# Last stage of a spectral layer in the matrices' place, its addend loaded at once, and the first matrices ahead of the token points

## Chip, cores, metric

The kernel runs on one core of a Trainium2 chip. The metric is the device time of one execution in microseconds; the median of three runs of the kernel before is 1634.19 us (1628.76 to 1636.43). Profiles come from one further execution each.

## What is computed

Two layers on an image `x` of 4 x 56 x 56 x 128 in float32. The first is neighbourhood attention with a residual. The second works on the same values as 4 sequences of 3136 tokens: a linear attention with a residual, then a spectral mixer with a residual. The change touches only the mixer, cut here to its core:

```python
t = t + attn(ln(t))
u = ln(t)
# one of four scales (here: all tokens, or the first half, ...) is picked by argmax(log_weights + gumbel)
Uf_p = rfft(u, n=8192);  Uf_m = rfft(u * sign, n=8192)
U_plus  = irfft(Vf * Uf_p)[:, :sl]          # 16 filters phi
U_minus = irfft(Vf * Uf_m)[:, :sl] * sign
out = einsum('btkd,k,kde->bte', U_plus, sigma**0.25, Mpp)
    + einsum('btkd,k,kde->bte', U_minus, sigma**0.25, Mpm)
t = t + out + autoregressive_part(u)
```

## The kernel before

**Phases.** `layers` computes the attention layers, the normalised tokens, the autoregressive part and everything that the spectral part needs. It leaves in DRAM: `td`, the result so far (what the last stage adds to), `xd`, the tokens transformed along rows, `vd`, the transformed filters, and `wd`, the filters' matrices. Its order of instructions on all engines is written out by a planner of its own. `spectral_layer` (L1419) then does the convolution as products between transforms, and `onto_the_rest` (L1680) transforms back along rows and adds the result to `td`. A second copy of all three stands under an `If` that these inputs do not take.

**The spectral layer's order.** There are 42 row frequencies `m1`, grouped in `UNITS`: one, then twenty pairs, then one. Only TensorE's order is written out (`tc.manual_schedule(engines={PE})`); on the other engines and queues the compiler orders instructions by priority and readiness. The step `step(s)` finishes unit `s-1` and prepares unit `s`:

- `load_tokens(m1)` (L1478) loads `xm` from `xd` by four DMAs on SP's queue; `points(m1)` turns it into points by 16 matmuls (32 records, L1490), which DVE, ScalarE and GpSimd copy into one of three `us` tiles (L1499 to L1503).
- `matrices(u, t, n)` (L1521) mixes the 16 x 2 filters' matrices `mats` with the filters' values `v` to the unit's matrices, which DVE and ScalarE copy into `gt` (L1531).
- `product` (L1541) multiplies points and matrices; ScalarE copies to `ys` (L1633).
- `regroup` stores `ys` to `yd` and loads it back as `yg` in another order (L1554 and L1560), `columns` transforms back along columns by 8 matmuls (L1569), ScalarE and DVE copy the two halves to `zs` (L182 and L184), and `store_columns` stores `zs` to `zd` (L1584). These DMAs are on SP's queue.

Before the first step, `mats` (2 MB) is loaded from `wd` by four DMAs on SP's queue (L1433), among the first loads of `v`, `tok` and `back` (`tables_of`, L1463). The first step loads the tokens of `m1 = 0` and 1, makes the points of `m1 = 0`, and then the matrices of unit 0; the second step begins with the first 32 matmul records of the next unit's matrices and then the first product.

The last frequency's chain has nothing after it in the layer: product, `ys`, `yd`, `yg`, `columns`, `zs`, `zd`.

**SBUF of the layer.** The pools `tabs`, `sp` and `sp1` lie one on the other. `sp1` holds what lives through the whole layer: `mats` (16 KB a partition), `gt` (112 KB) and three `us` (32 KB). All pools are freed together when the layer ends.

**The last stage.** `onto_the_rest` opens the pools `fin` and `ps_o`. It zeroes `onto` and the upper 64 rows of eight `z` tiles of 16 KB a partition (four sets of two halves `q`; L1687 and L1697, on DVE and GpSimd). Its eleven steps take 1, 1, 2, 4, 4, 4, 4, 4, 2, 1, 1 columns of the image from each half:

- two DMAs on ScalarE's queue load `tl` from `td` (L1709), 56 rows each, and two on SP's queue load the two `z` from `zd` (L1711), 84 rows from row 0;
- per column, four matmuls (8 records, L1719) with `onto` as weights give a PSUM tile `po` of 128 x 512, of which four rotate;
- DVE adds it, masked, to `tl` in two halves (L1728);
- two DMAs on ScalarE's queue store `tl` to the output (L1733).

Of the kernel before, what the change touches and what calls it, by code (L numbers as in the profile page):

```python
# [57 lines left out]
NS, BR = 2, H // 2  # L58
N1, N2, NM = 42, W, W // 2
# [74 lines left out]
def hybrid_kernel(  # L134
# [39 lines left out]
    hmask = keep.tile([P, 1], F32, name="hmask")  # L174
# [1244 lines left out]
    def spectral_layer():  # L1419


        with ExitStack() as ph:
            tabs = ph.enter_context(tc.tile_pool(name="tabs", bufs=2))
            sp = ph.enter_context(tc.tile_pool(name="sp", bufs=2))
            sp1 = ph.enter_context(tc.tile_pool(name="sp1", bufs=1))
            ps_g = ph.enter_context(tc.tile_pool(name="ps_g", bufs=1, space=bass.MemoryType.PSUM))


# [1 line left out]
            mats = sp1.tile([P, NQE, GE // NQE, C], F32, name="mats")  # L1430
            by_group = wd.rearrange("k (t g i) d -> g k t (i d)", t=NQE, g=NG)
            for g in range(NG):
                nc.sync.dma_start(  # L1433
                    mats[32 * g : 32 * (g + 1)].rearrange("k t i d -> k t (i d)"), by_group[g]
                )

# [151 lines left out]
            def bank():  # L1588
                turn[0] = (turn[0] + 1) % 8
                return ps_g.tile([P, 512], F32, tag=f"g{turn[0]}", name="pg")  # L1590
# [3 lines left out]
            def load_to(m1):  # L1594
                for m in range(len(xms), min(m1, N1 - 1) + 1):
                    xms[m] = load_tokens(m)
# [13 lines left out]
            def step(s):  # L1610


                one = UNITS[s - 1] if s else []
                two = UNITS[s] if s < len(UNITS) else []
                turns = NM // 4
                free = MQ * len(one)

                order = list(range(free, NQE)) + list(range(free)) if two else []
                need = lambda t: -(-NMQ * (t + 1) // 4) if t < free else 0
                done = 0  # L1620

                def make():
                    if order and need(order[0]) <= done:
                        t = order.pop(0)
                        for n in range(len(two)):
                            matrices(s, t, n)

                def use(q, ns):

                    py = bank().rearrange("p (n c) -> p n c", c=C)  # L1630
                    for i, n in enumerate(ns):
                        product(py[:, i], s - 1, us_of(one[q]), q, n)
                    nc.scalar.copy(ys[:, ns[0] : ns[-1] + 1], py[:, : len(ns)])  # L1633

                if not one:
                    load_to(1)
                    points(0)
                    while order:
                        make()
                elif len(one) == 1 and two:  # L1640
                    ys = sp.tile([P, turns, C], F32, name="ys")
                    for n in range(turns):
                        make()
                        use(0, [n])
                        done += 1
                        if n == 3:
                            points(two[0])
                    ygs[one[0]] = regroup(one[0], ys)
                    make()
                    points(two[1])  # L1650
                else:
                    waiting = list(ygs)
                    for q in range(len(one)):
                        ys = sp.tile([P, turns, C], F32, name="ys")
                        for n in range(0, turns, 2):
                            last = n + 1 == turns
                            if last and q == 0 and two:
                                points(two[0])
                            if last and q == len(one) - 1:
                                if q:  # L1660
                                    waiting.append(one[0])
                                for m1 in waiting:
                                    results(m1)
                            use(q, [n] if last else [n, n + 1])
                            done += len(range(n, min(n + 2, turns)))
                            make()
                        ygs[one[q]] = regroup(one[q], ys)
                    if len(two) == 2:
                        points(two[1])
                assert not order  # L1670

            with tc.manual_schedule(engines={mybir.EngineType.PE}):
                for s in range(len(UNITS) + 1):
                    if s + 1 < len(UNITS):
                        tables_of(UNITS[s + 1][0])
                    step(s)
                for m1 in list(ygs):
                    results(m1)

    def onto_the_rest():  # L1680

        with ExitStack() as ph:
            fin = ph.enter_context(tc.tile_pool(name="fin", bufs=4, reuse_waits="tile"))
            ps_o = ph.enter_context(tc.tile_pool(name="ps_o", bufs=4, space=bass.MemoryType.PSUM))

            onto = fin.tile([P, NS, 64], F32, name="onto", bufs=1)
            nc.vector.memset(onto, 0.0)  # L1687
            nc.scalar.dma_start(
                onto[: 2 * N1, :, :H], table["onto"].rearrange("p (s h) -> p s h", s=NS)
            )  # L1690
            zs = [
                [fin.tile([P, 4, NS, B * C], F32, name=f"z{q}{i}", bufs=1) for q in range(2)]
                for i in range(4)
            ]
            for i in range(4):
                for q, e in enumerate((nc.vector, nc.gpsimd)):
                    e.memset(zs[i][q][64:], 0.0)  # L1697
            rows_in = td.rearrange("b (h w) c -> h b w c", w=W)
            rows_out = ot.rearrange("b (h w) c -> h b w c", w=W)

            steps = (1, 1, 2, 4, 4, 4, 4, 4, 2, 1, 1)
            assert sum(steps) == W // 2
            for n, wc in enumerate(steps):
                w0 = sum(steps[:n])
                tl = fin.tile([P, B, max(steps), C], F32, name="tl")
                zin = []
                for q in range(2):
                    ws = slice(q * BR + w0, q * BR + w0 + wc)
                    nc.scalar.dma_start(tl[64 * q : 64 * q + H, :, :wc], rows_in[:, :, ws])  # L1709
                    z = zs[n % 4][q]  # L1710
                    nc.sync.dma_start(  # L1711
                        z[: 2 * N1, :wc], zd[ws].rearrange("w p s b e -> p w s (b e)")
                    )
                    zin.append(z)
                for i in range(wc):
                    po = ps_o.tile([P, B, C], F32, name="po2")
                    for s in range(NS):
                        for q in range(2):
                            nc.tensor.matmul(  # L1719
                                po[64 * q : 64 * (q + 1)].rearrange("p b c -> p (b c)"),  # L1720
                                onto[:, s],
                                zin[q][:, i, s],
                                start=(s == 0),
                                stop=(s == NS - 1),
                            )
                    for q in range(2):
                        at = slice(64 * q, 64 * q + H)
                        nc.vector.scalar_tensor_tensor(  # L1728
                            tl[at, :, i], po[at], hmask[at], tl[at, :, i], ALU.mult, ALU.add
                        )  # L1730
                for q in range(2):
                    ws = slice(q * BR + w0, q * BR + w0 + wc)
                    nc.scalar.dma_start(rows_out[:, :, ws], tl[64 * q : 64 * q + H, :, :wc])  # L1733

    unfit = keep.tile([1, 1], mybir.dt.int32, name="unfit")
    layers(False, unfit)
    bad = nc.values_load(unfit)
    spectral_layer()
    onto_the_rest()
    with tc.If(bad > 0):  # L1740
        layers(True, None)
        spectral_layer()
        onto_the_rest()


# [52 lines left out]
```

## Time and profile before

| | |
|---|---|
| median of the runs | 1634.19 us |
| the profiled execution's own time | 1643.69 us |
| its span, first to last instruction | 1641.8 us |
| TensorE busy in the span | 1436.1 us (87%) |
| DVE, ScalarE, GpSimd busy | 1015.0, 757.9, 411.8 us |
| bytes moved by DMA | 207.22 MB, mean 126 GB/s |
| the layer's first load (v) issued | 747.90 us |
| the first points' matmul | 769.14 us |
| end of the last product's copy to ys | 1488.5 us |
| first tl issue | 1500.76 us |
| last z issue | 1628.33 us |

A row of a group reads: line, engine, operation, output and inputs by the program's names, shape, count, then busy microseconds in all, mean nanoseconds of one, and the idle time of the engine before them with what ended it. `PEld` is the loading of weights, which overlaps the matmuls. `SPq` and `ACTq` are the queues of SyncE and ScalarE, that is, the issuing of DMAs, which is not counted as busy time. In the chain of waits each line is a start, a duration and what the time went to; a line that begins with DMA lasts from the end of the issue to what the landing released. The DMA share is the mean busy share of the core's 16 DMA engines. The last stage's matmuls as a group:

```
L1719 PE MATMUL po<-z,onto 128*64 128x512 f32 x224 | 76.6, 723 | 58.5 <-DMA z<-zd 57.4
```

### The profile page before, as it was taken

To read this page: it belongs to the slowest core of one execution; us is meant where nothing else is said; L and a number is where in the kernel's file an instruction comes from. 1 tells how busy PE (TensorE), PEld (TensorE's weight loads), DVE (VectorE), ACT (ScalarE), POOL (GpSimd) and SP (SyncE) were. 2 spreads that over 40 slices of the span, in tenths; PEclk is the share of its full clock that TensorE was granted. 3 is DMA by queue.
4 is the path that set the end of the run, shared out by engine and by line. 5 is a ranking of instruction groups with operands and counts; after the bars stand their busy time and mean duration, and the time that the engine had idled before them with its cause. 6 is when DMAs were issued, how large, how long until landed. Compare 5 with 4: busy or idle time off the path is not lost.

```text
span 1641.8 us, 60848 instructions
## 1 busy us (share of the span) xinstructions
PE 1436.1 (87%) x26361; PEld 1115.2 (68%) x26361; DVE 1015.0 (62%) x2069; ACT 757.9 (46%) x1610; POOL 411.8 (25%) x813
## 2 busy tenths in 40 slices
PE   4887879889999999883999999999999999992566
PEld 3665658756876776562888888888888888880212
DVE  3775668777876777541766666666666666643324
ACT  2333445346635534342666655666566556640000
POOL 5135327433754464240010011001010101003000
PEclk9698999999999999996999999999999999995788
DMA  6455455744434244257144444444444454435997
GB/s 174 106 109 105 89 86 109 162 122 118 117 111 125 66 121 124 74 157 202 48 113 119 106 123 126 127 108 125 122 126 108 121 132 115 107 93 139 225 252 238
DMA packets 274388, 207.22 MB, mean 126 GB/s; under 512 B 104704, under 2 KB 241056, under 8 KB 274112
## 3 DMA queue, kind: packets, MB, share of 16 engines
q1 hardware_dynamic: 261154, 189.63, 45.1%
q10 hardware_dynamic: 12958, 13.61, 3.1%
q8 instruction: 209, 3.42, 0.9%
q14 instruction: 67, 0.55, 0.1%
HBM read 115.52 MB, written 87.64 MB: 124 GB/s over the span
## 4 chain that ended last, share of the span: by engine, by line
PE 66%; DMA 14%; POOL 7%; DVE 6%; SPq 4%; issue 2%; ACT 1%; POOLq 0%; DVEq 0%; ACTq 0%
PE pg L1521 18%; PE pg L1541 17%; PE pg L1490 5%; PE results L1185 4%; PE scores L1155 3%; PE pg L1569 3%; PE bk L828 3%; SPq L230 2%; DMA z<-zd 2%; DMA tl<-td 2%; DMA out_dram<-tl 2%; PE bk L887 2%; PE bk L733 2%; PE bk L703 2%; PE bk L501 2%
## 5 line engine op out<-in xcount | busy, mean ns | idle before, releaser
L1531 DVE COPY gt<-pg 128x448 f32<-128x448 f32 x672 | 372.9, 617 | 225.6 <-PE pg L1521 225.5
L1531 ACT COPY gt<-pg 128x448 f32<-128x448 f32 x672 | 313.6, 555 | 101.3 <-PE pg L1521 101.1
L1521 PE MATMUL pg<-v,mats 32*128 32x224 f32 (+1 forms) x5632 | 308.9, 356 | 0.0
L1541 PE MATMUL pg<-gt,us 128*32 128x128 f32 x9408 | 297.7, 277 | 1.3 <-DVE gt L1531 1.3
L1541 PEld LDWEIGHTS pg<-gt,us 128*32 128x32 f32 x9408 | 256.5, 138 | 51.8 <-DVE gt L1531 45.4
L1521 PEld LDWEIGHTS pg<-v,mats 32*128 32x128 f32 x5632 | 250.5, 187 | 30.0 <-issue 28.5
L1502 POOL COPY us<-us 128x448 f32<-128x448 f32 x42 | 23.5, 560 | 667.0 <-DVE us L1499 611.9
L1171 ACT ACTIVATE e<-scores 126x768 f32<-126x768 f32 (+1 forms) x140 | 107.6, 769 | 116.8 <-PE scores L1155 93.3
L1175 DVE TENSOR_TENSOR e<-e,relb 126x768 f32<-126x768 f32 (+1 forms) x140 | 138.1, 987 | 23.7 <-ACT e L1171 23.0
L1199 DVE RECIPROCAL recs<-results 128x96 f32<-128x96 f32 (+1 forms) x140 | 99.4, 710 | 55.1 <-PE results L1185 53.9
L1719 PE MATMUL po<-z,onto 128*64 128x512 f32 x224 | 76.6, 723 | 58.5 <-DMA z<-zd 57.4
L1155 PEld LDWEIGHTS scores<-qT,kp 32*126 32x126 f32 (+1 forms) x2240 | 75.3, 187 | 50.0 <-ACT e L1171 25.2
L1155 PE MATMUL scores<-qT,kp 32*126 32x96 f32 (+1 forms) x2240 | 98.2, 291 | 11.8 <-ACT e L1171 11.6
L1490 PE MATMUL pg<-tok,xm 56*128 56x56 f32 x1344 | 87.2, 278 | 24.3 <-DMA xm<-xd 24.3
L1633 ACT COPY ys<-pg 128x256 f32<-128x256 f32 (+1 forms) x171 | 58.6, 343 | 106.2 <-PE pg L1541 102.3
L1490 PEld LDWEIGHTS pg<-tok,xm 56*128 56x128 f32 x1344 | 81.5, 191 | 36.8 <-issue 25.4
L1719 PEld LDWEIGHTS po<-z,onto 128*64 128x64 f32 x224 | 25.3, 163 | 110.5 <-issue 75.9
L1499 DVE COPY us<-pg 128x448 f32<-128x448 f32 x84 | 48.5, 620 | 67.2 <-PE pg L1490 67.2
L1728 DVE SCALAR_TENSOR_TENSOR tl<-po,hmask,tl 56x512 f32<-56x512 f32 x56 | 42.0, 750 | 74.0 <-PE po L1719 73.3
L828 PE MATMUL bk<-mu,ut 128*112 128x128 f32 x672 | 82.3, 281 | 2.2 <-POOL ut L812 1.6
L1185 PE MATMUL results<-e,v_sb 126*32 126x96 f32 (+1 forms) x2240 | 76.1, 255 | 9.3 <-DVE aT L1200 9.3
L1214 POOL TENSOR_TENSOR total<-total,recs 128x448 f32<-128x448 f32 x28 | 31.7, 1134 | 206.4 <-DVE recs L1199 206.4
(176 smaller groups left out, 1969.1 us busy)
## 6 DMA issues: line engine op xcount, KB each, us to landing
xd<-xs SPq DMA_DIRECT2D x56, 336.0 KB
xm<-xd SPq DMA_DIRECT2D x168, 112.0 KB
yd<-ys SPq DMA_DIRECT2D x168, 112.0 KB
yg<-yd SPq DMA_DIRECT2D x168, 112.0 KB
zd<-zs SPq DMA_DIRECT2D x168, 112.0 KB
v_sb<-vpad SPq DMA_DIRECT2D x224, 63.0 KB
z<-zd SPq DMA_DIRECT2D x10, 1344.0 KB
acc<-in_x_dram SPq DMA_DIRECT2D x28, 224.0 KB
```

Of the source, the lines that this page charges most:

```text
L828: nc.tensor.matmul(pt[:CP, g * C : (g + 1) * C], ut[:, t0 : t0 + 2 * CP - 1 : 2], mu[:, i, :], start=(i == 0), stop=(i == NAR - 1),)
L1155: nc.tensor.matmul(sp[:, h, c * nq : (c + 1) * nq], keys_of(x0, y0 + c * KH, KH)[hs], qTs[b, ty][hs, QR * x0 : QR * x0 + nq], start=True, ...
L1171: nc.scalar.activation(e.rearrange("k (h q) -> k h q", h=NH), sp, AF.Exp)
L1175: nc.vector.tensor_tensor(e, e, relb[qc].rearrange("k h c q -> k (h c q)"), ALU.mult)
L1185: nc.tensor.matmul(po[hs, i, :nq], ones[:kn] if i else v_sb[:kn, c, hs], e[:, h, c], start=(c == 0), stop=(c == 1),)
L1199: nc.vector.reciprocal(rec, po[:, 1, :nq])
L1490: nc.tensor.matmul(pu[p][:, HALF * k : HALF * (k + 1)], xm[at, k % B, k // B, :], tok[at], start=True, stop=True,)
L1521: nc.tensor.matmul(pg[g][:, cols * i : cols * (i + 1)], mats[rows, t, ni * n + i, :], v[rows], start=True, stop=True,)
L1531: copy(rows_of(u + 1, t)[:, : MQ * nm, :, e0 : e0 + ni], pg[g][:, : cols * ni].rearrange("p (i q c) -> p q c i", i=ni, q=MQ * nm),)
L1541: nc.tensor.matmul(py[32 * j : 32 * (j + 1)], us.rearrange("p c k m -> p (c k) m")[:, NSB * FIRST[p, c] : NSB * (FIRST[p, c] + 4), 4 * n + j],
L1633: nc.scalar.copy(ys[:, ns[0] : ns[-1] + 1], py[:, : len(ns)])
L1719: nc.tensor.matmul(po[64 * q : 64 * (q + 1)].rearrange("p b c -> p (b c)"), onto[:, s], zin[q][:, i, s], start=(s == 0), stop=(s == NS - 1),)
```

## The change

- `onto_the_rest` is gone as a function; its work stands at the end of `spectral_layer`, inside the layer's pools `tabs`, `sp` and `ps_g`. `sp1` has a stack of its own, which is closed after the last step but before the last frequency's `columns`; `fin` is opened in its place.
- All of `td` that the stage needs is loaded into one tile `rest` (56 KB a partition) by 14 DMAs of four columns each, on ScalarE's queue, and the additions and stores work in `rest`.
- `z` has three sets instead of four (`DEEP`), zeroed whole by GpSimd alone, and `z` and `onto` lie in rows 22 to 105 (`among`) instead of 0 to 83. `onto` is loaded after `rest` on the same queue.
- The last `results`, with its columns and stores, comes in the program after these loads and memsets.
- The `po` tiles come from the layer's eight rotating PSUM banks instead of four of a pool `ps_o`.
- `mats` is loaded on ScalarE's queue instead of SP's.
- In the first step the unit's matrices are made before the points of `m1 = 0`.

```diff
-            sp1 = ph.enter_context(tc.tile_pool(name="sp1", bufs=1))
+            matrices_in = ph.enter_context(ExitStack())
+            sp1 = matrices_in.enter_context(tc.tile_pool(name="sp1", bufs=1))
...
             for g in range(NG):
-                nc.sync.dma_start(
+                nc.scalar.dma_start(
                     mats[32 * g : 32 * (g + 1)].rearrange("k t i d -> k t (i d)"), by_group[g]
                 )
...
                 if not one:
                     load_to(1)
-                    points(0)
                     while order:
                         make()
+                    points(0)
...
                     step(s)
+
+            matrices_in.close()
+            fin = ph.enter_context(tc.tile_pool(name="fin", bufs=1, reuse_waits="tile"))
...
+            rest = fin.tile([P, B, BR, C], F32, name="rest")
+            half = [slice(64 * q, 64 * q + H) for q in range(2)]
+            for w0 in range(0, BR, 4):
+                for q in range(2):
+                    nc.scalar.dma_start(
+                        rest[half[q], :, w0 : w0 + 4], rows_in[:, :, q * BR + w0 : q * BR + w0 + 4]
+                    )
+            among = slice(P // 2 - N1, P // 2 + N1)
+            onto = fin.tile([P, NS, 64], F32, name="onto")
+            nc.gpsimd.memset(onto, 0.0)
+            nc.scalar.dma_start(
+                onto[among, :, :H], table["onto"].rearrange("p (s h) -> p s h", s=NS)
+            )
+            DEEP = 3
+            zin = [
+                [fin.tile([P, 4, NS, B * C], F32, name=f"z{q}{i}") for q in range(2)] for i in range(DEEP)
+            ]
+            for zs in zin:
+                for z in zs:
+                    nc.gpsimd.memset(z, 0.0)
+            with tc.manual_schedule(engines={mybir.EngineType.PE}):
                 for m1 in list(ygs):
                     results(m1)
...
-                tl = fin.tile([P, B, max(steps), C], F32, name="tl")
-                zin = []
                 for q in range(2):
-                    ws = slice(q * BR + w0, q * BR + w0 + wc)
-                    nc.scalar.dma_start(tl[64 * q : 64 * q + H, :, :wc], rows_in[:, :, ws])
-                    z = zs[n % 4][q]
                     nc.sync.dma_start(
-                        z[: 2 * N1, :wc], zd[ws].rearrange("w p s b e -> p w s (b e)")
-                    )
-                    zin.append(z)
+                        zin[n % DEEP][q][among, :wc],
+                        zd[q * BR + w0 : q * BR + w0 + wc].rearrange("w p s b e -> p w s (b e)"),
+                    )
                 for i in range(wc):
-                    po = ps_o.tile([P, B, C], F32, name="po2")
+                    po = bank()
...
                         nc.vector.scalar_tensor_tensor(
-                            tl[at, :, i], po[at], hmask[at], tl[at, :, i], ALU.mult, ALU.add
+                            rest[half[q], :, w0 + i],
+                            po[half[q]].rearrange("p (b c) -> p b c", b=B),
+                            hmask[half[q]],
+                            rest[half[q], :, w0 + i],
+                            ALU.mult,
+                            ALU.add,
                         )
                 for q in range(2):
-                    ws = slice(q * BR + w0, q * BR + w0 + wc)
-                    nc.scalar.dma_start(rows_out[:, :, ws], tl[64 * q : 64 * q + H, :, :wc])
+                    nc.scalar.dma_start(
+                        rows_out[:, :, q * BR + w0 : q * BR + w0 + wc], rest[half[q], :, w0 : w0 + wc]
+                    )
```

More of the change, by code (lines that the diff above doesn't have):

```diff
@@ L1676, in spectral_layer @@
                     step(s)
+            matrices_in.close()
+            fin = ph.enter_context(tc.tile_pool(name="fin", bufs=1, reuse_waits="tile"))
+            rows_in = td.rearrange("b (h w) c -> h b w c", w=W)
+            rows_out = ot.rearrange("b (h w) c -> h b w c", w=W)
+            rest = fin.tile([P, B, BR, C], F32, name="rest")
[5 more added lines that the diff above has]
+                    )
@@ L1677, in spectral_layer @@
+            with tc.manual_schedule(engines={mybir.EngineType.PE}):
                 for m1 in list(ygs):
                     results(m1)
[L1680 to L1689, printed above, removed]
-            )
[L1691 to L1699, printed above, removed]
@@ L1701, in onto_the_rest @@
             steps = (1, 1, 2, 4, 4, 4, 4, 4, 2, 1, 1)
-            assert sum(steps) == W // 2
+            assert sum(steps) == BR
             for n, wc in enumerate(steps):
                 w0 = sum(steps[:n])
-                tl = fin.tile([P, B, max(steps), C], F32, name="tl")
-                zin = []
                 for q in range(2):
-                    ws = slice(q * BR + w0, q * BR + w0 + wc)
-                    nc.scalar.dma_start(tl[64 * q : 64 * q + H, :, :wc], rows_in[:, :, ws])
-                    z = zs[n % 4][q]
@@ L1719, in onto_the_rest @@
                             nc.tensor.matmul(
-                                po[64 * q : 64 * (q + 1)].rearrange("p b c -> p (b c)"),
+                                po[64 * q : 64 * (q + 1)],
                                 onto[:, s],
-                                zin[q][:, i, s],
+                                zin[n % DEEP][q][:, i, s],
                                 start=(s == 0),
@@ L1726, in onto_the_rest @@
                     for q in range(2):
-                        at = slice(64 * q, 64 * q + H)
                         nc.vector.scalar_tensor_tensor(
-                            tl[at, :, i], po[at], hmask[at], tl[at, :, i], ALU.mult, ALU.add
+                            rest[half[q], :, w0 + i],
[4 more added lines that the diff above has]
+                            ALU.add,
                         )
                 for q in range(2):
-                    ws = slice(q * BR + w0, q * BR + w0 + wc)
-                    nc.scalar.dma_start(rows_out[:, :, ws], tl[64 * q : 64 * q + H, :, :wc])
+                    nc.scalar.dma_start(
+                        rows_out[:, :, q * BR + w0 : q * BR + w0 + wc], rest[half[q], :, w0 : w0 + wc]
+                    )
     unfit = keep.tile([1, 1], mybir.dt.int32, name="unfit")
@@ L1738, in hybrid_kernel @@
     spectral_layer()
-    onto_the_rest()
     with tc.If(bad > 0):
@@ L1742, in hybrid_kernel @@
         spectral_layer()
-        onto_the_rest()
 def kernel(**inputs):
```

## Prediction

> **What bounds the kernel now.** I read the page first, then the busy times by stretch around both edited places, the chain of waits there, the issue times, and the queues' own waits. The profiled execution took 1643.69 us (span 1641.8); the middle, 787 to 1480 us, is TensorE work that the change does not touch. Two stretches are touched: the start of the spectral layer (748 to 787) and everything from the last product on (1488 to 1641.8).
>
> The last stage by stretch (columns: stretch, length, then busy us of PE, PEld, DVE, ACT, POOL, PE clock, DMA share, GB/s):
>
> ```profile
> 1488.00:1501.00 13.00, 3.22 (x12) 0.61 (x8) 0.29 (x1) 0.61 (x2) 0.18 (x1) 0.50 0.42 106
> 1501.00:1508.00 7.00, 0.00 (x0) 0.00 (x0) 4.02 (x3) 0.25 (x1) 7.00 (x3) 0.50 0.53 144
> 1508.00:1516.00 8.00, 0.00 (x0) 0.00 (x0) 6.01 (x2) 0.00 (x0) 6.68 (x2) 0.50 0.89 204
> 1516.00:1548.00 32.00, 15.67 (x44) 6.14 (x46) 10.71 (x11) 0.00 (x0) 0.00 (x0) 0.67 0.92 224
> 1556.00:1568.00 12.00, 0.34 (x3) 0.16 (x4) 0.00 (x0) 0.00 (x0) 0.00 (x0) 0.70 0.92 212
> 1568.00:1592.00 24.00, 20.73 (x59) 6.46 (x60) 10.50 (x14) 0.00 (x0) 0.00 (x0) 0.87 0.90 287
> ```
>
> From 1508 on the DMA share stays near 0.9 while every engine has idle time: the stage is DMA-bound. It runs near 205 to 225 GB/s where it mostly loads, and at 287 where 2 KB stores run beside the loads. So loads are the limit, and stores largely ride along. From 1488 to 1508 the engines are mostly idle: the last unit's chain runs alone, and then POOL's zeroing stands in front of the first load:
>
> ```profile
> 1492.16 2.09 DMA yd<-ys
> 1494.40 0.33 SPq L1560
> 1494.78 2.63 DMA yg<-yd
> 1497.40 0.14 issue
> 1497.54 3.10 PE pg L1569 x8
> 1500.82 0.58 POOL z L1697
> 1501.51 2.76 issue
> 1504.27 3.52 POOL z L1697
> 1507.82 0.32 SPq L1711
> 1508.20 9.80 DMA z<-zd
> ```
>
> The loads themselves, KB each, and what SP's issues wait for (us in total, times, longest):
>
> ```profile
> z<-zd SPq DMA_DIRECT2D x10, 1344.0 KB
> ...
> tl<-td ACTq DMA_DIRECT2D x10, 448.0 KB
> ```
>
> ```profile
> SPq L1711 <- DMA tl<-td: 44.4, 5, 17.7
> SPq L1711 <- DMA out_dram<-tl: 36.6, 6, 10.5
> ```
>
> With the smaller steps (8 of 336 and 4 of 672 KB; 8 of 112 and 4 of 224 KB) that is 19.27 MB of z and 6.42 MB of tl. The last two lines say that z's issue waits for transfers of the other queue with which it shares no data; I take it that completions share semaphores, so an issue waits for an older transfer.
>
> The start of the layer:
>
> ```profile
> 747.21 4.51 DMA xd<-xs
> ...
> 753.78 11.37 DMA mats<-wd
> ...
> 765.17 4.77 DMA xm<-xd
> ...
> 770.07 3.63 PE pg L1490 x30
> 773.70 6.59 PE pg L1521 x132
> 780.33 6.48 PE pg L1521 x155
> 786.81 1.04 PE pg L1541 x32
> ```
>
> The matrices land at 765.15, then the last token DMA that waited for them, then points, matrices and, at 786.8, the first product.
>
> [...]z's first 672 KB, issued at 1507.8 behind seven tl loads on the other queue, landed only at 1518.0.[...]
>
> **The change part by part.**
>
> *Check of the load rate.* From 1500.8 (first tl issue) to 1633.7 (last z landed) 25.69 MB take 132.9 us, 193 GB/s. The first 7 us are poor ([...]z waiting for zeros); from 1508 on it is some 25.1 MB in 125.7 us, 200. I use 197.
>
> *Rest loaded at once.* The loads keep their 6.42 MB but can start when the last product has read gt (1488.2), not at 1500.8. Fourteen issues on ACT at 0.43 to 0.80 us each (rows of tl's issues) are 6 to 11 us. Behind them on ACT stand the half of zs that ACT copies (1500.66 before) and all stores; at 11 us the issues end just before that copy. If later ones wait for earlier landings (2.3 us each), ACT is held until about 1507; that goes into the gap below. The last ys copy stands ahead of them by program order.
>
> *The chain beside it.* yd (448 KB in 512-byte packets), yg and zd now share engines with 2 KB packets. [...]11 us where it took about 3.6, +7. yg with 4 KB packets +1, zd with 2 KB packets +2. z can start at about 1507.8 + 10 = 1518, by 1526 if the chain's issues also wait for rest's landings. This costs nothing while rest is still loading: alone it needs 6.42/0.197 = 33 us, to 1522, later with the chain among it.
>
> *The sum.* Loads from 1489.2: 25.69 MB plus yg's 0.46 are 26.15/0.197 = 132.7 us, to 1621.9. A gap where rest is done and z is not yet flowing, or where onto (queued behind rest) or ACT is late: 0 to 12, I take 3. After the last z the tail is 8.1 us as before (1633.7 to 1641.8). End 1633.0: **8.8 us gained**.
>
> *Smaller edits, at nothing.* Zeroing: six memsets of 3.5 us ([...]taken the same for 128 rows as for 64) plus onto's, 1489 to 1510 on POOL, which is free after its last us copy at 1457.8; z comes at 1518. Without that cover z1 and z2 would be late by some us. Four sets become three: loading four columns takes 14 us, their matmuls 8.7 to 12.3, so a set is back after some 28 us and needed after 42. Eight PSUM banks for four: PE waited 1.0 us for them. `among`: 0, with -10 and +5 as ends, from 98 us of z loads at 10% faster or 5% slower.
>
> *Matrices first, on ACT's queue.* mats' four issues waited for the landing of xd at 751.7 and will again; ACT is idle then, and SP loses 2.6 us of issue. But 2.1 MB now share the engines with v, tok and back (0.6 MB) and some token packets: about 3.0 MB at 206 to 215 GB/s is 14 to 14.5 us from 752.4, so PE can start at about 767, against 769.1 with points before. Then 256 matrix matmuls (12.2: part at the low clock, as in 773.7 to 786.8), points 2.0 at full clock (the later points at 796.18 take 1.93), and until us is copied by DVE and POOL 2.6, in part under the next unit's first 32 matmuls: product at 783.9 instead of 786.8. **2.9 us gained**, ends -1 (mats at 771) and +6 (mats at 764). points(0) later delays the third token load behind it on SP, and the next tables after that, by some 10 us; they are needed at 809 and later.
>
> Together 11.7 us: 1643.7 becomes 1632.0. The profiled execution stands 9.5 us above the median of 1634.19; I carry the difference over: **1622.5 us**.
>
> **Rivals.**
> *Chain starved (19%).* If packets and shared waits hold yd until rest is in (1522), z follows 13.6 us later (1494.25 to 1507.82 now), at 1535.6, plus 97.8 for z and 8.1: 1641.5. Only the start's 2.9 is left: 1631. For it: SP's 44.4 us behind tl. Against: yd is issued 2 us after rest begins.
> *Rest not early (7%).* If the new pool waits for more than gt, rest starts at 1501; 1631 too, or little below.
> *Loads behind stores (17%), slower.* With three sets, and if an issue waits for the previous step's store to land (36.6 us of such waits now), each step of four columns takes matmuls 8.7, DVE 1.5, store 3.2 (alone, at 287 GB/s) to 9.7 (at some 95 beside loads), latency 2: 15.4 to 21.9 instead of 14. At the middle 4.7 more on five steps is 23.5: 1646. It decides once a step passes 14 us. Against it: without tl on ACT, fewer transfers stand between two z loads.
>
> **How the numbers follow.** The likeliest case (57%) runs from 1611 (no gap, a quick start, some gain from `among`) to 1628 (gap 8). The two neutral cases lie near 1631, up to 1641 if the chain is later still. 1611 to 1641 leaves out the slower case and a little below. A measurement of this kernel can tell about 0.5%, 8.2 us. Faster: 57% less 3 that end within 8.2 us, 54%. Same: 19 + 7 + 3 = 29%. Slower: 17%.
>
> **What would show it.** rest<-td issued from about 1488 on ACT and DMA share near 0.9 at once; yd's landing stretched to some 10 us; z's first issue at 1515 to 1526; no low DMA share between 1526 and the last z; the last z at about 1625 less the start's gain; PE's first matrices near 767. I am wrong if z loads at another rate than 197, if the DMA share drops between steps, or if z's first issue is after 1530.

## The result, and the profile after

Before: 1634.78 us, the median of 12 runs (1628.76 to 1641.89). After: 1626.53 us, the median of 12 (1618.88 to 1630.47). The ratio is 0.9937, 95% interval [0.9917, 0.9956]: 10.3 us off the time, between 7.2 and 13.6 (the two medians by themselves lie 8.3 us apart). The profiled execution of the changed kernel took 1630.07 us, with a span of 1628.0.

The two traces give three parts. The start runs from the last issue of xd to the first matmul of the first product; "last product" is here and below the time at which the last matmul of the last product begins (1487.75 before, 1481.86 after):

| part | before | after |
|---|---|---|
| last issue of xd to the first product (the start) | 39.5 | 41.7 |
| first product to last product (the middle) | 701.0 | 700.6 |
| last product to the end of the span (the end stretch) | 154.0 | 146.1 |

The rest of the difference between the two traces lies ahead of xd (747.2 against 739.6 us), where the change touches nothing; I put it down to the execution. So the middle stands still, the end stretch is 7.9 us shorter, and the start, which was to get shorter, got 2.2 longer.

The end stretch of the changed kernel by stretch (columns as in the prediction's first table):

```profile
1482.00:1485.00 3.00, 0.13 (x8) 0.00 (x0) 0.00 (x0) 0.27 (x1) 2.71 (x2) 0.99 0.55 104
1485.00:1498.00 13.00, 0.00 (x0) 0.00 (x0) 0.00 (x0) 0.00 (x0) 13.00 (x5) 0.50 0.97 249
1498.00:1511.00 13.00, 3.30 (x8) 0.61 (x8) 0.67 (x1) 0.58 (x1) 5.20 (x2) 0.50 0.93 195
1511.00:1522.00 11.00, 0.00 (x0) 0.00 (x0) 0.02 (x1) 0.00 (x0) 0.00 (x0) 0.50 0.82 203
1522.00:1546.00 24.00, 15.15 (x37) 4.87 (x38) 6.00 (x8) 0.00 (x0) 0.00 (x0) 0.78 0.87 239
1546.00:1570.00 24.00, 19.43 (x56) 5.84 (x55) 8.89 (x12) 0.00 (x0) 0.00 (x0) 0.92 0.91 272
1570.00:1594.00 24.00, 18.44 (x56) 5.84 (x54) 10.35 (x15) 0.00 (x0) 0.00 (x0) 0.86 0.90 272
```

Before, the DMA share stood at 0.42 and 0.53 for 20 us after the last product. Now it is at 0.97 within 3 us of it, and stays between 0.82 and 0.93 while the chain runs. POOL's zeroing (20.9 us in the first three rows) ends ahead of the first z. The DMA engines are nearly full, and the chain beside the loads pays for it. Its instructions, as SP issues them:

```profile
1481.59 3.35 SPq L1586 DMA_DIRECT2D zd<-zs  x4
1485.05 5.88 SPq L1556 DMA_DIRECT2D yd<-ys  x4
1498.27 1.61 SPq L1562 DMA_DIRECT2D yg<-yd  x4
1511.08 4.05 SPq L1586 DMA_DIRECT2D zd<-zs  x4
1521.66 7.49 SPq L1716 DMA_DIRECT2D z<-zd  x7
```

From yd to yg 13.2 us, where it took 3.8 (1490.65 to 1494.40); from yg to zd 12.8 instead of 7.1; from zd to the first z 10.6 instead of 6.3. The first z comes 39.8 us after the last product, where it came 20.1 us after it. The chain of waits goes through the same transfers, and then through one more:

```profile
1483.31 7.29 DMA zd<-zs
1490.62 7.59 DMA yd<-ys
...
1499.49 8.60 DMA yg<-yd
...
1508.60 13.02 DMA onto<-onto
...
1521.66 3.26 DMA z<-zd
```

onto, 36.8 KB queued behind the 14 loads of rest, landed at 1521.62, 0.2 us after the last zd (1521.45), and was the last thing that the first z's issue waited for. Had it come later, it would have been the bound (that happens in an experiment below). The last load of rest landed at 1521.5: up to the first z there was rest to load.

The start, as the chain of waits of the changed kernel has it:

```profile
739.59 4.00 DMA xd<-xs
...
743.69 9.26 DMA mats<-wd
...
752.97 0.31 SPq L1480
...
753.32 5.44 DMA xm<-xd
...
758.78 6.99 DMA mats<-wd
...
765.81 6.40 PE pg L1523 x120
```

A load of mats (on ACT) holds a load of xm (on SP), for 8.3 us in the table of SP's waits, and the load of xm behind it holds the last load of mats. In the trace each issue's record names the semaphore on which its landing shows: the 781 loads and stores from 735 us on, on both queues, name eight between them, 100 to 107, and none of them left before the transfer that had its semaphore before it had landed. The load of xm at 752.97 has the semaphore of the first load of mats; the third load of mats (747.24) has that of back, the last one (758.78) that of the next load of xm. Each of the three left 0.02 us after that landing. So ACT needs 15.7 us to issue four DMAs, and the matrices are there 22.1 us after xd has landed (743.6 to 765.77). Before, they took 13.4 (751.7 to 765.15).

### The profile page after: what moved, and what is told of

Its sections match the earlier page's. It is cut to its first block, busy times and chain, and to the rows that moved or that the text cites. A ratio compares the mean times of both kernels' runs of the same rounds, so it can differ in the third digit from the quotient of the medians.

```text
span 1628.0 us, 60810 instructions
## 1 busy us (share of the span) xinstructions
PE 1434.3 (88%) x26361; PEld 1114.6 (68%) x26361; DVE 1000.4 (61%) x2064; ACT 757.7 (47%) x1610; POOL 417.8 (26%) x816
## 4 chain that ended last, share of the span: by engine, by line
PE 64%; DMA 15%; DVE 7%; POOL 6%; SPq 5%; issue 2%; ACT 1%; ACTq 0%; DVEq 0%; POOLq 0%
PE pg L1523 18%; PE pg L1543 17%; PE pg L1492 5%; SPq L230 4%; PE results L1185 4%; PE bk L828 3%; DMA z<-zd 3%; PE scores L1155 3%; PE pg L1571 3%; PE bk L887 2%; DMA out_dram<-rest 2%; PE bk L501 2%; DVE e L1175 2%; PE bk L733 1%; POOL hna L547 1%
## 5 line engine op out<-in xcount | busy, mean ns | idle before, releaser
L1155 PE MATMUL scores<-qT,kp 32*126 32x96 f32 (+1 forms) x2240 | 98.5, 292 | 11.7 <-ACT e L1171 11.6
L1724 PE MATMUL pg<-z,onto 128*64 128x512 f32 x224 | 75.1, 681 | 36.5 <-DMA z<-zd 34.8
L1732 DVE SCALAR_TENSOR_TENSOR rest<-pg,hmask,rest 56x512 f32<-56x512 f32 x56 | 42.0, 750 | 70.4 <-PE pg L1724 69.6
L1724 PEld LDWEIGHTS pg<-z,onto 128*64 128x64 f32 x224 | 23.9, 150 | 87.9 <-issue 66.7
L828 PEld LDWEIGHTS bk<-mu,ut 128*112 128x112 f32 x672 | 80.7, 192 | 4.0 <-POOL ut L812 1.9
```

What stands on the lines that cost most here:

```text
L828: nc.tensor.matmul(pt[:CP, g * C : (g + 1) * C], ut[:, t0 : t0 + 2 * CP - 1 : 2], mu[:, i, :], start=(i == 0), stop=(i == NAR - 1),)
L1155: nc.tensor.matmul(sp[:, h, c * nq : (c + 1) * nq], keys_of(x0, y0 + c * KH, KH)[hs], qTs[b, ty][hs, QR * x0 : QR * x0 + nq], start=True, ...
L1724: nc.tensor.matmul(po[64 * q : 64 * (q + 1)], onto[:, s], zin[n % DEEP][q][:, i, s], start=(s == 0), stop=(s == NS - 1),)
```

## Experiments

What had to be told apart: for the **start**, whether the matrices come late because they share the engines with other loads, or because loads on two queues wait for each other. For the **end**, whether the stage is bound by its bytes, so that a late chain is covered as long as something is loading, or pays for the chain's delay. And what `among` and the stores are worth. Each expectation says what its own theories are. Ratios are to the kernel before on the same chip; the four of a group share a chip.

A trace is one execution, and the same code differs from one to the next: the new last stage, with no edit to it, has end stretches from 134.7 to 146.1 us in five traces, the old one 154.0 and 161.1 in two. A few us between two single traces therefore prove nothing by themselves; they count where the ratios say the same.

### First group: the parts by themselves

**The start alone**: the kernel before with these edits only, the first in the loop that loads mats.

```
-                nc.sync.dma_start(
+                nc.scalar.dma_start(
...
-                    points(0)
                     while order:
                         make()
+                    points(0)
```

> The kernel before with the two start edits alone: mats on ScalarE's queue, and the first matrices ahead of the first points. From the last landing of xd to the first product it took 35.0 us before and 37.7 after. If the start's loss is a property of these edits: about 37.7 here, the end stretch (last product's end to the span's end) as before, 153.6, and a time 2 to 3 us above before. Rival: the loss in the one trace after is chance, and this stretch is 32 to 35 here, as the prediction had it.

1644.92 us against 1638.98, ratio 1.0022 [1.0001, 1.0043]: the start alone costs 3.6 us (0.2 to 7.0). In its trace the start takes 40.4 us, 0.9 more than before; the end stretch, which these edits do not touch, takes 161.1 instead of 154.0. The seven traces with these edits have starts of 40.0 to 41.7 us, the two without them 39.5 and 38.6: 1.8 us on the average. So both have the same sign, and the size is some 2 to 4 us. Its chain of waits shows the same interlocking with the old last stage behind it:

```profile
748.31 8.09 DMA mats<-wd
...
756.77 5.57 DMA xm<-xd
...
762.36 6.08 DMA mats<-wd
...
768.48 6.74 PE pg L1521 x120
```

**The last stage alone**: the changed kernel with the two edits above undone.

> The changed kernel with the start put back (mats on SyncE's queue, points first): only the new last stage. If the gain comes from the last stage alone: start 35.0, end stretch about 146 (153.6 before), and 8 to 10 us below before, 2 to 3 below the changed kernel. Rival: part of the measured gain comes from elsewhere; then this kernel is slower than the changed one.

1624.29 us, ratio 0.9903 [0.9872, 0.9934]: 15.9 us gained (10.8 to 21.0), more than the 8 to 10 expected. Its end stretch is 141.0 us, and its first z comes 39.3 us after the last product, so the chain is as late here.

**Matrices first, but on SP**: the changed kernel with one word changed, in the loop that loads mats.

```
-                nc.scalar.dma_start(
+                nc.sync.dma_start(
```

> The changed kernel with mats back on SyncE's queue, matrices still ahead of the points. Theory 1, the queues hold each other up (mats' issues on ScalarE wait for landings of token loads on SyncE and the other way round): mats land about 13.4 us after xd as before, and the first product follows 15.5 us later, so the start stretch is about 29 us instead of 37.7, and the time 8 us below the changed kernel. Theory 2, the order costs it (points no longer hidden): the stretch stays at 36 to 38.

1616.96 us, ratio 0.9873 [0.9836, 0.9909], the fastest of all. From xd's last issue to the first product it takes 32.7 us, 9.0 less than in the changed kernel's trace and 6.8 less than before. The same bytes are loaded beside the same other loads as in the changed kernel; only the queue of mats differs. So sharing was not the cause. The first matrices in earnest run at 754.0, 14.0 us after xd landed (740.0). SP issues the four at once:

```profile
740.08 2.60 SPq L1435 DMA_DIRECT2D mats<-wd  x4
...
746.11 9.76 SPq L1480 DMA_DIRECT2D xm<-xd  x8
```

against ACT in the changed kernel:

```profile
743.69 15.68 ACTq L1435 DMA_DIRECT2D mats<-wd  x4
```

The xm loads are still strung out (9.76 us for eight), but mats does not stand behind them any more, and points are needed only after the matrices.

**Rows from 0**: the changed kernel with z and onto in rows 0 to 83.

```
-            among = slice(P // 2 - N1, P // 2 + N1)
+            among = slice(0, 2 * N1)
```

> The changed kernel with z and onto in rows 0 to 83 again instead of 22 to 105; no other instruction changes. If the rows matter, z's loads alone run near 197 GB/s as before instead of the 215 seen after, and the end stretch grows from 145.9 by 3 to 7 us. If they don't, as the prediction took it: 145 to 147, and the higher rate has another cause.

1632.64 us, ratio 0.9957 [0.9938, 0.9976]. In its z phase:

```profile
1519.30:1545.00 25.70, 16.16 (x38) 4.98 (x39) 6.00 (x8) 0.00 (x0) 0.00 (x0) 0.77 0.87 218
1545.00:1570.00 25.00, 18.97 (x60) 5.82 (x58) 10.44 (x14) 0.00 (x0) 0.00 (x0) 1.00 0.91 254
1570.00:1595.00 25.00, 18.61 (x59) 5.97 (x60) 9.80 (x15) 0.00 (x0) 0.00 (x0) 1.00 0.90 257
```

At the DMA shares of the changed kernel (0.87, 0.91, 0.90) these move 218, 254 and 257 GB/s where that moves 239, 272 and 272. The last-stage-alone kernel, on the same chip as this one, moves more still:

```profile
1545.00:1570.00 25.00, 22.32 (x64) 7.69 (x64) 10.00 (x14) 0.00 (x0) 0.00 (x0) 0.89 0.91 278
1570.00:1595.00 25.00, 20.00 (x64) 6.33 (x62) 10.98 (x15) 0.00 (x0) 0.00 (x0) 0.93 0.90 304
```

The z loads are issued over 94.9 us, against 91.6 in the changed kernel and 86.6 in the last-stage-alone kernel. By themselves the 19.27 MB of z come in at 193 GB/s here, from the first issue to the last landing, and at 210 in the last-stage-alone kernel. The end stretch is 146.9, against 141.0 in the latter; the expected 149 to 153 was counted from the changed kernel's trace, on another chip. Against the last stage alone the ratio is 0.54% higher, 8.8 us; 1.4 (by the two traces) to 3.6 us (by the ratio of the start alone) of it are the start. So the rows are worth 5 to 7 us, loosely: the two ratios' intervals (0.19% and 0.31% each way) leave some 6 us on either side. That there is an effect rests on the rates, which in all five traces of the new last stage with rows 22 to 105 are above those of this one.

### Second group: the chain and the queues

**The changed kernel again**, as control on this chip.

> The changed kernel itself, unchanged, on the chip of the next three, to compare their stages with. Stretches as in its trace: last product to first z issue 39.8 us, z's loads 91.6, end stretch 146.1; on a chip whose loads run faster some 140. Time 0.5 to 1% below before.

1628.37 us, ratio 0.9909 [0.9874, 0.9944]; end stretch 143.4, first z 39.7 us after the last product.

**Rest after yg**: a copy on POOL of a few numbers from the last yg into rest makes all loads of rest wait.

```
+            for q in range(2):
+                nc.gpsimd.tensor_copy(
+                    rest[half[q], 0, 0:BR:4, 0:1].rearrange("p w c -> p (w c)"), ygs[N1 - 1][half[q], 0, 0 : BR // 4]
+                )
```

> The changed kernel with a copy of seven numbers a row from the last yg into rest, which the loads of rest then have to wait for: the chain's yd and yg run without rest beside them, and rest starts about 9 us later. Theory 1, the stage is bound by what has to be loaded: first z issue at about 22 us after the last product instead of 40, but the end stretch stays within 4 us of the control, more likely 2 longer. Theory 2, the delayed chain is what costs: the end stretch shrinks by 10 us or more.

1640.99 us, ratio 1.0004 [0.9985, 1.0022]; end stretch 158.0, 14.6 longer than the control's. Without rest beside them, yd and yg are quick again:

```profile
1489.41 1.98 SPq L1556 DMA_DIRECT2D yd<-ys  x4
1493.14 1.60 SPq L1562 DMA_DIRECT2D yg<-yd  x4
1528.08 7.53 SPq L1586 DMA_DIRECT2D zd<-zs  x4
```

3.7 us from yd to yg, so it was rest that stretched them. But the experiment changed two things more than it meant to: the copy stood on POOL behind memsets of z, so rest began 21.7 us after the last product and not 9, and ACT's half of the last zs copy stood behind rest's 14 issues, so zd came 41.6 us after the last product and the first z 55.4, where 22 was expected. It shows how much the order on POOL and ACT weighs, and does not decide between bytes and chain. The third group repeats it without both.

**Rest on two queues**: the upper half of rest through GpSimd's queue.

```
-                    nc.scalar.dma_start(
+                    (nc.scalar, nc.gpsimd)[q].dma_start(
```

> The changed kernel with the upper half of rest (rows 64 to 119) loaded from GpSimd's queue, beside the lower half on ScalarE's[...]. If rows on one side limit a load, as the rows of z suggest, rest comes in at 240 GB/s or more instead of about 195, the first z is issued some 6 to 8 us earlier, and the end stretch shrinks by 4 to 8. If reading itself is the limit, rest takes as long as in the control and nothing moves.

1630.67 us, ratio 0.9938 [0.9910, 0.9965]; end stretch 144.2, no gain. Rest did come in faster. By stretch, first the control, then this kernel:

```profile
1500.00:1512.00 12.00, 3.31 (x8) 0.61 (x8) 0.69 (x1) 0.59 (x1) 4.22 (x2) 0.50 0.93 198
1512.00:1528.00 16.00, 1.78 (x4) 0.63 (x6) 0.00 (x0) 0.00 (x0) 0.00 (x0) 0.50 0.80 210
```

```profile
1500.00:1512.00 12.00, 0.00 (x0) 0.00 (x0) 0.00 (x0) 0.00 (x0) 11.18 (x4) 0.50 0.96 272
1512.00:1528.00 16.00, 3.16 (x8) 0.61 (x8) 0.69 (x1) 0.59 (x1) 0.00 (x0) 0.50 0.39 98
```

But the chain stood still meanwhile, as its chain of waits shows:

```profile
1485.48 10.53 DMA zd<-zs
...
1496.02 19.36 DMA yd<-ys
```

28.0 us from yd's issue to yg's instead of 13.6. When rest was in, z could not start yet, and the DMA share fell to 0.39: here the late chain did cost, since nothing was left to load beside it. With a third queue in use yd's last transfer took 19.4 us where the control's took 7.8; why it took so long was not shown.

**Stores on GpSimd's queue**: the output stores leave ACT's queue.

```
-                    nc.scalar.dma_start(
+                    nc.gpsimd.dma_start(
```

> The changed kernel with the stores to the output on GpSimd's queue. z's issues no longer wait for stores (30.8 us of such waits in the changed kernel, the longest 12.9). If those waits cost time, z's loads take 5 or more us less and the end stretch shrinks; if, as the prediction took it, other loads in flight hide them, less than 3 us changes.

1630.44 us, ratio 0.9919 [0.9883, 0.9955]; end stretch 144.1 against 143.4. In the changed kernel SP's queue waits for stores that share no data with z:

```profile
SPq L1716 <- DMA z<-zd: 49.0, 9, 7.2
SPq L1716 <- DMA out_dram<-rest: 30.8, 4, 12.9
```

With the stores on the third queue these waits, 29.0 us in the control's trace, are gone. What takes their place is the ordinary wait for a free z buffer, and one at the end:

```profile
SPq L1716 <- PE pg L1724: 58.2, 15, 10.6
...
SPq L1802 <- DMA out_dram<-rest: 10.3, 1, 10.3
```

The z issues end after 81.2 us instead of 89.4 and the last z lands 129.3 us after the last product instead of 134.1. But the stores that are then still to go take 14.9 us instead of 9.3, and the sum stays. A 31 us entry in the table of waits was worth nothing that these runs can tell (the two ratios differ by 0.1%, each is good to some 0.4%). It fits a stage bound by the bytes of loads and stores together.

### Third group: the same question without the side effects

**Control**: the kernel with mats on SP, on a third chip.

> The control of this group: the changed kernel with mats back on SP's queue and the first matrices still ahead of the points. Both theories: 0.987 of before as measured on another chip, some 16 to 20 us; last product to the first z issue 38 to 41 us, yd to yg's issue about 13 us, last product to the end of the span 137 to 143 us.

1619.91 us against 1639.87, ratio 0.9884 [0.9851, 0.9916]; end stretch 134.7, first z 37.7 us after the last product, start 33.5. The gain of the first group repeats. All four kernels of this group have mats on SP.

**All of rest after yg**: the copy on DVE, and the last zs copies both on DVE.

```
-                    evacuate(zs[:, p], pz[p])
+                    (nc.vector.tensor_copy if m1 == N1 - 1 else evacuate)(zs[:, p], pz[p])
...
+            for q in range(2):
+                nc.vector.tensor_copy(
+                    rest[half[q], 0, 0:BR:4, 0:1].rearrange("p w c -> p (w c)"),
+                    ygs[N1 - 1][half[q], 0, 0 : (BR - 0) // 4],
+                )
```

> As the control, but all 14 loads of rest wait for the last yg (a 7-element copy per row from it on DVE), and the last unit's two zs copies are both on DVE, so that nothing of the chain stands behind rest's issues on ACT. Theory 1 (the stage is bound by its bytes; the chain may run late as long as something is loading): the 9 us in which rest does not load are lost, less what yd and yg gain by having the engines alone (9 us earlier): end stretch within 4 us of the control, first z at about 30 us after the last product. Theory 2 (the chain's delay is what the stage pays): first z at about 30 instead of 40 us, and the end stretch 8 to 10 us shorter than the control's.

1625.57 us, ratio 0.9918 [0.9886, 0.9950], 5.7 us above the control. Here the chain is quick: the first z is issued 27.0 us after the last product, 10.7 sooner than in the control. (onto, which waits for nothing, goes ahead of rest here.) Yet the end stretch is 142.9, 8.2 us longer. By stretch:

```profile
1475.90:1487.10 11.20, 1.62 (x16) 0.51 (x8) 1.16 (x2) 0.27 (x1) 10.61 (x5) 0.50 0.48 128
1487.10:1503.20 16.10, 1.78 (x7) 0.10 (x3) 4.73 (x3) 0.00 (x0) 10.35 (x3) 0.50 0.87 200
1503.20:1519.20 16.00, 7.90 (x20) 3.01 (x20) 3.00 (x4) 0.00 (x0) 0.00 (x0) 0.64 0.91 242
```

and the control:

```profile
1476.20:1491.20 15.00, 0.39 (x8) 0.00 (x0) 0.00 (x0) 0.27 (x1) 14.47 (x6) 0.50 0.87 229
1491.20:1503.20 12.00, 3.12 (x8) 0.61 (x8) 0.00 (x0) 0.00 (x0) 6.45 (x2) 0.50 0.93 211
```

The first 11.2 us run at a DMA share of 0.48 where the control has 0.87: 11.2 x (0.87 - 0.48)/0.87 = 5.0 us of transfers lost, and nothing later gives them back; the other 3 us of the trace are not accounted for. The two ratios' intervals overlap, so that a loss of 5.7 us is likely and not sure; but a gain of 8 to 10 is outside them. The theory of bytes had allowed 4 us and is a little off in size; the theory that the chain's delay is what the stage pays had called for 8 to 10 us less, and falls.

**Most of rest after yg**: as the last one, with the first 6 of 14 loads free to go.

```
-                    rest[half[q], 0, 0:BR:4, 0:1].rearrange("p w c -> p (w c)"),
-                    ygs[N1 - 1][half[q], 0, 0 : (BR - 0) // 4],
+                    rest[half[q], 0, 12:BR:4, 0:1].rearrange("p w c -> p (w c)"),
+                    ygs[N1 - 1][half[q], 0, 0 : (BR - 12) // 4],
```

> As the last one, but the first 6 of rest's 14 loads (12 of 28 columns, 2.75 MB, some 14 us of loading) wait for nothing and only the other 8 wait for yg. Theory 1: the engines are never without loads, so the end stretch is 0 to 4 us shorter than the control's, with the first z about where the control has it or up to 5 us sooner. Theory 2: yd still runs beside rest, so the first z stays near 40 us and the end stretch stays within 2 us of the control's.

1626.55 us, ratio 0.9911 [0.9877, 0.9945], 6.6 us above the control by the medians and 4.4 by the ratios; the first z comes at 34.3 us, and the end stretch is 152.6. Both theories missed. The trace says why:

```profile
1490.80:1503.20 12.40, 3.05 (x8) 0.61 (x8) 3.71 (x4) 0.00 (x0) 5.26 (x2) 0.50 0.60 143
...
1519.20:1533.00 13.80, 3.98 (x10) 1.41 (x12) 0.26 (x1) 0.00 (x0) 0.00 (x0) 0.50 0.56 143
```

```profile
1508.88 8.18 SPq L1721 DMA_DIRECT2D z<-zd  x6
1518.87 0.96 ACTq L1702 DMA_DIRECT2D onto<-onto  x1
1529.02 2.83 PE L1729 MATMUL pg<-z,onto 128*64 128x512 f32 x6 [32.13 <-DMA z<-zd]
```

The first six loads of rest were in before yg came, so the DMA share fell to 0.60. onto stood behind the delayed loads of rest on ACT until 1511.0, and was issued only at 1518.87. The first matmul, which reads it, began at 1529.0. The line names z for that wait; I take it that onto ended it, since the first z were issued from 1508.88 on, 10 us ahead of onto. SP's issues of z meanwhile waited 12.9 us for PE, and the share fell to 0.56. So this run weighs onto's place, and does not answer the question it was made for.

**Most after yg, on two queues**: as the last one, rest's upper half on GpSimd's queue and half of z's zeroing on DVE.

```
-                    nc.scalar.dma_start(
+                    (nc.scalar, nc.gpsimd)[q].dma_start(
...
-                for z in zs:
-                    nc.gpsimd.memset(z, 0.0)
+                for q, z in enumerate(zs):
+                    (nc.vector, nc.gpsimd)[q].memset(z, 0.0)
```

> As the last one, but the upper half of rest's loads goes through GpSimd's queue and the zeroing of the z tiles is shared by DVE and POOL. Theory 1: rest comes in faster (272 instead of 198 GB/s were seen with two queues), but yd is held longer beside two other queues (28 us were seen with all 14 loads beside it, 15 to 20 with 6): end stretch from 4 us shorter to 4 us longer than the control's. Theory 2: the first z at 45 us or later, and the end stretch 5 us or more longer.

1621.69 us, ratio 0.9895 [0.9857, 0.9934]: not to be told from the control. Its trace has the first z 42.3 us after the last product and an end stretch of 147.8, 13.1 longer than the control's; but that execution took 5.3 us more than the median of its kernel, and the control's 7.0 less than its own. The ratios fit the first theory and the trace's end stretch the second, so this run decides nothing. No arrangement of rest beat the plain one.

## Why the prediction was right

Forecast 11.7 us of gain, 1622.5 us; measured 10.3 (7.2 to 13.6), 1626.53, inside the range, with the sign of the likeliest case. What carried it is the step of the early loads, which was right in mechanism and size. That the total came so close is in part luck: two other terms were off by about as much, in opposite directions.

**The start, forecast 2.9 us shorter, measured 3.6 longer** (0.2 to 7.0, alone; 1.8 by the traces): wrong in sign, and beyond the 1 us longer that was kept as the worse end. The step that failed is "2.1 MB now share the engines ... PE can start at about 767": it let all four loads of mats leave at 752.4 and divided bytes by a rate. They left over 15.7 us, because xm waited for mats and the last mats for xm. Where they leave at once (mats on SP) PE starts 14.0 us after xd's landing, against the 15.3 that the division gave: the rate was right and the issue times were not. The prediction itself had read such a wait in the last stage (SP's 44.4 us behind tl) and did not ask where else two queues now ran side by side. Moving the matrices ahead was a good step: with mats on SP it gains some 6 to 7 us of the start (39.5 to 32.7 and 33.5).

**Rest at once, forecast 8.8 us shorter, with nothing for `among`.** The last stage alone gained 15.9 (10.8 to 21.0). With the rows put back to 0, and against the start alone on the same chip (ratios 0.9957 and 1.0022), it gained 0.65%, 10.7 us (6 to 15). So the step of the early loads was right; `among` was the mis-sized term, some 5 to 7 us and not 0, inside the ends kept for it. The 0 was an estimate; the trace of before has z in rows 0 to 83 alone. The rates of 254 and 257 GB/s there against 278 and 304 in rows 22 to 105 on the same chip have the sign of a gain; what makes it was not shown.

In the traces the sum holds closely. The run with rows from 0, which is what the sum assumed, had its last z landed 137.4 us after the last product (forecast 137.1, with the gap). In the changed kernel's trace loads began 0.4 us after it (forecast 1.4), the last z landed at 136.5, and the tail took 9.6 (forecast 8.1); with the rows' gain in it, this single execution was rather slow there (134.1 in the control of the second group, 131.3 in the last stage alone). One reading behind the sum does not stand. That "stores largely ride along" is too strong: with the stores on a third queue the last z landed 4.8 us sooner, and the end did not come sooner.

**The chain, forecast 10 us later, measured 20.** From yd to yg it lost 9.5 (forecast 7), from yg to zd 5.7 (forecast 1), from zd to z 4.3 (forecast 2). Two things were missed. Issues waited: yd's four took 5.9 us instead of 2.0, since the last one has the semaphore of the zd of the frequency before, itself slow beside rest (7.29 us in the chain). For the same reason the 14 issues of rest took 26.2 us, not 6 to 11. And the size of the pieces, from which the 7, 1 and 2 were estimated, with no trace that showed it to matter, did not decide: from last issue to landing yd with 512-byte pieces took 7.6 us instead of 2.1, yg with 4 KB pieces 8.6 instead of 2.9. The delay cost little or nothing here: the last of rest landed as the first z was issued, so the forecast's "this costs nothing while rest is still loading" held to the end. The third group's first pair shows the same, where a chain 10.7 us sooner did not make the stage shorter, since rest was later.

**The rivals.** The chain was starved about as that rival said (z first at 39.8 us after the last product, the rival's 47.8), but its time of 1631 did not follow: z's delay was covered. Rest was early, so the second is out. Loads did wait behind stores (30.8 us), as the slower rival had it, but the five steps of four columns did not become 23.5 us longer together: the DMA share stays at 0.84 to 0.91, and taking the waits away moved the end by 0.7 us.

**What was set to nothing.** Zeroing cost nothing: six memsets of 128 rows took 20.8 us on POOL, 3.5 each as with 64 rows, and were done at 1503.2, z at 1521.7. Three sets for four were not tried by themselves; z's issues waited 3.2 us in all for PE. The gap, taken as 3 us, is about 1 us (a share of 0.82 instead of some 0.9 from 1511 to 1522).

## What to carry to other kernels

Where a stage is bound by its bytes, start the bytes at once and let the short chain beside them be late (here the first z came 19.7 us later, and the end stretch was 7.9 us shorter). Ask whether something is loading at every moment: once the bytes that wait for nothing are in, the late chain costs (the DMA share fell to 0.39 with rest on two queues). Keep small loads that everything needs out from behind the large ones (onto, behind 14 loads of rest, landed 13.0 us after its issue, 0.2 us after the last zd). Before a load is moved to another queue, look at what will be in flight on both: where the queues share semaphores, their issues can wait for each other's landings, and a second queue was slower than one here (15.7 us for four issues instead of 2.6). A large entry in the table of waits is worth what the bound leaves of it, which can be nothing (here some 30 us of waits, and an end that moved by 0.7).

## What the runs showed of the hardware

- Four issues of mats took 2.6 us on SP and 15.7 us on ACT, the last two of them behind landings of the other queue that share no data with them. The issues' records go with that: the 781 transfers of the layer name eight semaphores on both queues, and none left before the last user of its semaphore had landed. With the stores on GpSimd's queue SP's waits for stores ahead of z, 29.0 us in the control's trace, were gone.
- Small transfers were much slower beside a queue of large loads, whatever their pieces: 112 KB from issue to landing took 2.0 to 3.0 us with no rest or tl beside them, and 5.4 to 8.6 us beside one queue of it, with pieces of 512 bytes (yd), 2 KB (zd) and 4 KB (yg). With the waits of the issues, yd's 448 KB took 3.7 to 4.0 us alone, 12.8 to 13.6 beside one queue of rest and 28.0 beside two, from its first issue to the first of yg. Why they were slower was not separated.
- The same z loads moved more in rows 22 to 105 than in rows 0 to 83, stores among them, at equal DMA share: 278 against 254 and 304 against 257 GB/s on one chip; 239 against 218, 272 against 254 and 272 against 257 with the changed kernel's trace from another.
